# A triangle product's layer norm in a pipeline of its own, and the output units' first thirteen steps made within it

## The chip, the cores and the metric

The kernel runs on one core of a Trainium2 chip. A core has a matrix engine (TensorE, PE in the profile; its weight loads are PEld), VectorE (DVE), ScalarE (ACT), GpSimd (POOL) and SyncE (SP, which here only issues transfers), and 16 DMA engines. Each engine works through its own list of instructions in order; an instruction that waits holds up all behind it on its engine. SBUF is the on-chip memory of 128 partitions, PSUM the small accumulator memory in eight banks that TensorE writes. The metric is device microseconds (us) of one execution, as the median of several runs.

## The reference

Everything is float32; x is 1 x 512 x 512 x 64. Layer 0 is a gated triangle product, layer 1 a Fourier filter of 12 x 12 modes:

```python
xn = _ln(_gn(x), norm_w, norm_b)
left  = (xn @ left_w  + left_b)  * mask * sigmoid(xn @ lgate_w + lgate_b)
right = (xn @ right_w + right_b) * mask * sigmoid(xn @ rgate_w + rgate_b)
out_gate = sigmoid(xn @ ogate_w + ogate_b)
out = einsum('bkjd,bkid->bijd', left, right)        # per channel: a 512 x 512 product over k
out = _ln(out, onorm_w, onorm_b) @ out_w + out_b    # norm over the 64 channels
x = x + out * out_gate
x = x + spectral_filter(_gn(x))
```

The mask is the outer product of a 0/1 row of length 512 with itself, so only rows and columns that it keeps (at most K = 256 of them here) take part in the product; elsewhere the norm of zeros leaves only a bias row.

## The kernel before, in words

The kernel is one function, compact (L633). It has these stages, by the times of its profile: the statistics of the first group norm and the gather of the kept columns (to about 160 us); the gated left and right sides (to some 425 us); the triangle product channel by channel (425 to 591 us, L995, stored to DRAM as tri_d, L1003); then the loop of L1288, which the change rewrites (593 to some 1410 us); and the inverse transform with the final output (to the end).

The loop of L1288 runs over steps s, from -13 to 335. k = s // 8 and n = s % 8. It is one pipeline for two kinds of work:

- **Product steps**, s = 0 to 63. A step takes 1024 tokens, as 128 partitions by 8 groups of 64 channels. centered (L1143) multiplies a piece of the product with the matrix both, whose left half subtracts the channel mean and whose right half is the output projection (y_ps, L1153, sixteen matmuls). ScalarE squares the centered half into sq_c (L1173) and copies the projected half to SBUF (xt_c, L1174). VectorE sums the squares of two steps (summed, L1178) into PSUM. Once per eight steps ScalarE takes the root (L1184, in step n = 5) and VectorE its reciprocal (L1358, n = 7). VectorE multiplies the projected tokens with it (L1366), GpSimd adds the bias row for two steps at a time (L1373), and SP stores the pair, 512 KB, to u_d in DRAM (L1378).
- **Unit steps**, s = 64 to 319: 32 output units of eight steps. A unit is 64 columns by 128 rows of x, gathered earlier (L649). TensorE transposes (t_ps, L1133), ScalarE subtracts the group mean into xt_c (L1135), TensorE makes the centered values (c_ps) and the output gate (w_ps, both L1140); ScalarE squares (L1171), VectorE sums (L1178), and root and reciprocal follow as above. VectorE scales the gate (L1369) and adds its bias (L1375), ScalarE takes the sigmoid (L1316), GpSimd multiplies with u, read back from u_d, or with the bias row where the mask is 0 (gated, L1204), and adds x (added, L1208). VectorE takes the statistics for the second group norm (L1263), and TensorE begins the Fourier transform (L1235).

In every turn of the loop the early part of a step (transpose of step s + 13, centering, square and sum of step s + 12) is issued beside the late part (scaling) of step s. LEAD = 13 is that distance, for both kinds. So the first 13 turns only fill the pipeline with product steps, and during the last 12 product steps the early part already belongs to the units.

The whole block is in a manual schedule: each engine gets its instructions in the order in which the program issues them. The sums, the factors (reciprocals) of the product, the bias rows for VectorE and the group sums all lie in one PSUM tile, scratch, which is one bank (L1101). The projected values and the units' two results have two PSUM buffers each; the product's pool of PSUM is closed and replaced by the units' pools at s = 52 (L1302).

The queue of SP carries, in order, the loads of the product (load_product, L1121, 512 KB for two steps, four buffers) and the stores of u. The load for pair q is issued three pairs ahead of its projection. After the last store, load_u (L1195) reads u back for each second unit in 32 transfers of 64 KB.

The SBUF area xc is divided into eight places of 16 KB per partition: places 0, 1, 3 hold the first three units, which were gathered long before; place 6 holds the product's four load buffers; places 5 and 6 later hold u; places 4 and 2 the fourth and fifth unit; place 7 is free until the first unit's transform is saved.

Of the kernel before, what the change touches and what calls it, by code (L numbers as in the profile page):

```python
# [9 lines left out]
F32 = mybir.dt.float32  # L10
I32 = mybir.dt.int32
AF = mybir.ActivationFunctionType
ALU = mybir.AluOpType
# [33 lines left out]
def conv_preact_kernel(ctx: ExitStack, tc: tile.TileContext, t: dict):  # L47
# [585 lines left out]
    def compact(fc):  # L633
# [324 lines left out]
        with held:  # L958
# [59 lines left out]
            LEAD = 13  # L1018
            RING = 5
# [3 lines left out]
            with tc.manual_schedule(), tc.tile_pool(name="late", bufs=1) as lp:  # L1023
# [63 lines left out]
                with tc.tile_pool(name="np_x", bufs=LEAD + 2) as tp, tc.tile_pool(name="np_q", bufs=2) as sqp, tc.tile_pool(  # L1087
# [20 lines left out]
                    factors = [scratch[:, i, SIZE * 8 :] for i in range(2)]  # L1108
# [16 lines left out]
                    def transpose(s):  # L1125
                        k, n = divmod(s, SIZE)
                        if k < first:
                            return
# [14 lines left out]
                    def centered(s):  # L1143
                        if s >= first * SIZE:
                            return times(ps_c, "c_ps", s, center_x)
# [8 lines left out]

                        xts[s] = tp.tile([P, 4, P], F32, name="xt_c")
                        return ps

                    def raw(s):
                        return xts[s].rearrange("p h (i c) -> p (h i) c", c=C).rearrange("p (h i) c -> p h i c", h=2)
# [5 lines left out]
                    def squared(s, cps):  # L1165
                        n = s % SIZE
                        if n % 2 == 0:
                            sqs[s // 2] = sqp.tile([P, 16, C], F32, name="sq_c")
                        sq = sqs[s // 2][:, 8 * (n % 2) : 8 * (n % 2) + 8, :]
                        if s >= first * SIZE:  # L1170
                            nc.scalar.activation(sq, cps, AF.Square)  # L1171
                        else:
                            nc.scalar.activation(of_pair(sqs[s // 2], n % 2), cps[:, :, :, :C], AF.Square)  # L1173
                            nc.scalar.copy(raw(s), cps[:, :, :, C:])  # L1174
# [112 lines left out]
                    loaded = 0  # L1287
                    for s in range(-LEAD, total_g + 2 * SIZE):  # L1288
# [5 lines left out]

                        while loaded < K // 8 and 2 * loaded - LEAD - 5 <= s:
                            load_product(loaded)
                            loaded += 1
# [3 lines left out]
                        if s + LEAD - 1 == first * SIZE:  # L1301
                            products.close()  # L1302
                            ps_c = products.enter_context(tc.tile_pool(name="np_c", bufs=2, space=PSUM))
                            ps_w = products.enter_context(tc.tile_pool(name="np_w", bufs=2, space=PSUM))
                        if 0 <= s < total_g:
                            wps = raw(s) if k < first else times(ps_w, "w_ps", s, gate_x)
                            del xts[s]
                        if 0 <= s + LEAD - 1 < total_g:
                            cps = centered(s + LEAD - 1)
# [7 lines left out]
                        if n == 5 and 0 <= k + 1 < first + len(units):  # L1317
                            root(k + 1)
# [36 lines left out]
                        if 0 <= s + LEAD - 2 < total_g and (s + LEAD - 2) % 2 == 1:  # L1355
                            summed(s + LEAD - 2)
                        if n == 7 and k + 1 in rss:
                            nc.vector.reciprocal(factors[(k + 1) % 2] if k + 1 < first else rss[k + 1], rss[k + 1])  # L1358
                        if wps is not None:
# [3 lines left out]
                            if k < first:  # L1363
                                rs = factors[k % 2][:, 16 * c : 16 * c + 16].rearrange("p (h e i) -> p h e i", h=2, e=2)
                                rs = rs[:, :, odd].unsqueeze(3).to_broadcast([P, 2, 4, C])
                                nc.vector.tensor_mul(of_pair(z, odd), wps, rs)  # L1366
                            else:
# [261 lines left out]
```

## Time and profile before

| what | value |
|---|---|
| median of 3 runs | 1745.74 us (1744.92 to 1746.58) |
| the profiled execution itself | 1740.37 us |
| its span, first to last instruction | 1738.6 us |
| mean granted TensorE clock | 0.899 |
| busy over the span: PE, DVE, ACT, POOL | 1534.2, 1410.2, 949.4, 933.2 us |
| product projections y_ps, first and last start | 597.1 and 692.4 us |
| product scaling L1366, first and last start | 616.5 and 711.7 us |
| units' first centering c_ps, first gate w_ps | 693.8 and 710.9 us |
| units' scaling L1369, first and last start | 713.6 and 1406.8 us |
| product: sum L1178, scaling L1366, reciprocal of 64 columns L1358 | 1.21, 0.68, 0.56 us each |
| product: square L1173, copy L1174, root L1184 | 0.60, 0.59, 0.31 us each |
| bias addition on GpSimd L1373, 32 of them | 2.37 us each |
| load of two product steps, issue to landing | 6.4 us (median) |
| store of a pair of u, issue to landing | 2.6 us (median) |

A row of the profile's groups gives the line, engine, operation, the tile written and the tiles read, the count, the busy time and the mean of one, and the idle time of the engine just before, with what ended it. Two neighbouring instructions on one engine may overlap by a few tenths of a us at their ends, so the distance from start to start, read in order of time, is the better price of an instruction on a busy engine. The times of windows and timelines count from the span's start.

### The profile page before, as it was taken

To read this page: it belongs to the slowest core of one execution; us is meant where nothing else is said; L and a number is where in the kernel's file an instruction comes from. 1 tells how busy PE (TensorE), PEld (TensorE's weight loads), DVE (VectorE), ACT (ScalarE), POOL (GpSimd) and SP (SyncE) were. 2 spreads that over 40 slices of the span, in tenths; PEclk is the share of its full clock that TensorE was granted. 3 is DMA by queue.
4 is the path that set the end of the run, shared out by engine and by line. 5 is a ranking of instruction groups with operands and counts; after the bars stand their busy time and mean duration, and the time that the engine had idled before them with its cause. 6 is when DMAs were issued, how large, how long until landed. Compare 5 with 4: busy or idle time off the path is not lost. (4 is left out here: it accounts for less than half of the span.)

```text
span 1738.6 us, 32562 instructions
## 1 busy us (share of the span) xinstructions
PE 1534.2 (88%) x10926; PEld 1232.6 (71%) x10926; DVE 1410.2 (81%) x2967; ACT 949.4 (55%) x1740; POOL 933.2 (54%) x695
## 2 busy tenths in 40 slices
PE   6877899998999877999999999999999868998771
PEld 6776666655999766988888988898889735664340
DVE  7999788886555488899999999999999976785441
ACT  3766777764333377877777777777777632101000
POOL 4666111110000068799999999999999871111110
PEclk9999999999999899999999999999999876555555
DMA  7999378877999689577777767777777699999998
GB/s 293 420 419 418 85 240 285 300 243 288 306 304 301 234 280 331 180 264 264 247 249 262 250 242 249 262 249 246 248 267 245 200 341 423 426 426 426 426 428 363
DMA packets 189330, 518.48 MB, mean 298 GB/s; under 512 B 36416, under 2 KB 103232, under 8 KB 146272
## 3 DMA queue, kind: packets, MB, share of 16 engines
q1 hardware_dynamic: 154864, 295.71, 47.0%
q0 software_dynamic: 30816, 218.38, 33.9%
q10 hardware_dynamic: 3472, 2.20, 0.5%
q8 instruction: 89, 1.46, 0.3%
q14 instruction: 89, 0.73, 0.1%
HBM read 311.60 MB, written 204.60 MB: 297 GB/s over the span
## 5 line engine op out<-in xcount | busy, mean ns | idle before, releaser
L1140 PE MATMUL w_ps<-gate_x,xt_c 128*128 128x128 f32 x2048 | 280.3, 281 | 31.2 <-DVE z_t L1369 29.6
L1208 POOL TENSOR_TENSOR xc<-xc,z_t 128x1024 f32<-128x1024 f32 x127 | 301.2, 2372 | 8.0
L1140 PEld LDWEIGHTS w_ps<-gate_x,xt_c 128*128 128x128 f32 x2048 | 252.1, 194 | 47.7 <-DVE z_t L1369 46.0
L1140 PE MATMUL c_ps<-center_x,xt_c 128*128 128x128 f32 x2048 | 276.8, 279 | 1.2 <-ACT xt_c L1174 0.6
L1140 PEld LDWEIGHTS c_ps<-center_x,xt_c 128*128 128x128 f32 x2048 | 252.8, 194 | 3.6 <-ACT xt_c L1135 2.5
L1535 PE MATMUL l_ps<-xc,rinv 24*128 24x512 f32 x512 | 206.1, 1096 | 32.5 <-DVE xc L1542 20.4
L1263 DVE BATCH_NORM_STATS2 stats2c<-xc 128x6 f32<-128x128 f32 x1024 | 220.5, 278 | 8.5 <-POOL xc L1208 8.5
L1178 DVE TENSOR_REDUCE scratch<-sq_c 128x16 f32<-128x1024 f32 x160 | 194.5, 1216 | 23.4 <-ACT sq_c L1173 18.8
L1316 ACT ACTIVATE z_t<-z_t 128x1024 f32<-128x1024 f32 x128 | 135.5, 1059 | 133.4 <-DVE z_t L1375 132.7
L1373 POOL TENSOR_TENSOR z_t<-z_t,bias_row_out 128x1024 f32<-128x1024 f32 x32 | 75.7, 2367 | 241.9 <-DMA xc<-tri_d 220.7
L1535 PEld LDWEIGHTS l_ps<-xc,rinv 24*128 24x128 f32 x512 | 118.5, 296 | 114.9 <-DVE xc L1542 61.7
L1135 ACT ACTIVATE xt_c<-t_ps,ab_xc 128x512 f32<-128x512 f32 x256 | 175.9, 687 | 9.6 <-PE t_ps L1133 8.7
L1369 DVE TENSOR_TENSOR z_t<-w_ps,rs_n 128x512 f32<-128x512 f32 x256 | 172.0, 672 | 4.5 <-PE w_ps L1140 4.4
L1171 ACT ACTIVATE sq_c<-c_ps 128x512 f32<-128x512 f32 x256 | 150.5, 588 | 29.4 <-PE c_ps L1140 28.9
L1375 DVE TENSOR_TENSOR z_t<-z_t,scratch 128x1024 f32<-128x1024 f32 x128 | 156.3, 1221 | 10.7 <-ACT rs_n L1184 3.7
L1204 POOL TENSOR_TENSOR z_t<-z_t,xc 128x1024 f32<-128x1024 f32 x64 | 151.6, 2368 | 15.0 <-ACT z_t L1316 14.8
L777 DVE BATCH_NORM_STATS2 stats1c<-x_ps 128x6 f32<-128x512 f32 x256 | 156.2, 681 | 3.3 <-PE x_ps L776 2.9
L1133 PE MATMUL t_ps<-c_ident,xc 128*128 128x128 f32 x1024 | 157.4, 276 | 0.0
L1542 DVE TENSOR_TENSOR xc<-xc,l_ps 128x512 f32<-128x512 f32 x176 | 110.5, 682 | 55.6 <-DMA xc<-x_h,dst_i 47.0
L1133 PEld LDWEIGHTS t_ps<-c_ident,xc 128*128 128x128 f32 x1024 | 117.6, 141 | 51.6 <-issue 51.3
L1204 POOL TENSOR_TENSOR z_t<-z_t,bias_row_out 128x1024 f32<-128x1024 f32 x63 | 150.0, 2381 | 6.2 <-ACT z_t L1316 6.0
L751 ACT COPY xc<-xg 128x128 f32 x352 | 105.0, 298 | 51.6 <-DMA xg<-in_x,src_i 40.7
(231 smaller groups left out, 2540.8 us busy)
## 6 DMA issues: line engine op xcount, KB each, us to landing
x_h<-xc SPq DMA_DIRECT2D x64, 1024.0 KB, 8.1
out_x<-xc SPq DMA_DIRECT2D x44, 1024.0 KB, 32.5
sides_d<-o_c SPq DMA_DIRECT2D x64, 512.0 KB, 5.7
xc<-u_d SPq DMA_DIRECT2D x512, 64.0 KB, 2.4
out_x<-lx_t SPq DMA_DIRECT2D x20, 1024.0 KB, 39.5
left_raw<-sides_d SPq DMA_DIRECT2D x64, 256.0 KB, 4.4
right_raw<-sides_d SPq DMA_DIRECT2D x64, 256.0 KB, 4.2
tri_d<-tri_t SPq DMA_DIRECT2D x64, 256.0 KB, 3.6
```

Of the source, the lines that this page charges most:

```text
L777: nc.vector.bn_stats(stats[:, 0, 16 * (jc % quarter) + 4 * r + c, :], ps.rearrange("p i k -> p (i k)"))
L1133: nc.tensor.transpose(tps[:, i, :], flat[:, o : o + P], ident)
L1135: nc.scalar.activation(xts[s], tps, AF.Identity, bias=ab1[:, 2:3])
L1140: nc.tensor.matmul(ps[:, 2 * i : 2 * i + 2, :], xts[s][:, i, :], w, start=True, stop=True)
L1171: nc.scalar.activation(sq, cps, AF.Square)
L1178: nc.vector.tensor_reduce(totals[k % 2][:, 8 * (n - 1) : 8 * (n + 1)], sqs.pop(s // 2), AX.X, ALU.add)
L1204: nc.gpsimd.tensor_mul(zs[k, c], zs[k, c], u)
L1208: nc.gpsimd.tensor_add(xr, xr, zs.pop((k, c)))
L1263: nc.vector.bn_stats(st[k // 4][:, g, k % 4, :], x_of(k)[:, :, 2 * g : 2 * g + 2])
L1369: nc.vector.tensor_mul(z[:, 8 * odd : 8 * odd + 8, :], wps, rs)
L1375: nc.vector.tensor_add(z, z, bias_ps["ogate"].unsqueeze(1).to_broadcast([P, 16, C]))
L1535: nc.tensor.matmul(ps.rearrange("p j o -> p (j o)"), rinv[h, b, :], it[h], start=True, stop=True, tile_position=(32 * g, 0),)
```

## The change

The product steps leave the common loop and get one of their own, with steps p from -6 to 63:

- The projection of step p + 6 is issued beside the scaling of step p (LATE = 6 instead of 13). ScalarE copies the projected half into one of eight buffers in place 4 (tokens) and the scaled results are made in places 2 and 5 (scaled, four buffers of two pairs).
- The root and the reciprocal are made for four steps at a time (ROOT = 4), on 32 columns: the root is issued at the start of steps p = -1, 3, 7 and so on, the reciprocal at the end of the same steps. Sums and factors have two buffers each, all in the same PSUM tile, scratch.
- A store takes four steps (1 MB) instead of two and is issued three steps after their last scaling step; the last one follows the loop.
- Of the units' thirteen early steps, four (transpose, centering, square, sum) are made ahead of the loop, with centering in the buffers of the projection; eight within it, two in each of four groups of sixteen steps, with centering in the buffers of the transposes; and the thirteenth is only transposed, at p = 58. The squares of these steps go to place 7.
- The first unit's root is issued at p = 26 and its reciprocal at p = 29.

The old loop then begins at s = 64, with its pipeline already full, and does only unit steps; their code is otherwise the same.

```diff
+            LATE = 6
+            ROOT = 4
...
-                    factors = [scratch[:, i, SIZE * 8 :] for i in range(2)]
+                    sums_p, factors = [
+                        [scratch[:, i, (SIZE + ROOT * j) * 8 : (SIZE + ROOT * (j + 1)) * 8] for j in range(2)] for i in range(2)
+                    ]
+                    tokens = place(4).rearrange("p n c -> p (n c)")
+                    tokens = [tokens[:, i * N : (i + 1) * N].rearrange("p (h i c) -> p h i c", h=2, c=C) for i in range(8)]
+                    scaled = [place(i)[:, r * JC : (r + 1) * JC] for i in (2, 5) for r in range(2)]
+                    squares = [place(7)[:, 16 * i : 16 * i + 16] for i in range(4)]
...
+                    def squared_pair(p, ps):
+                        if p % 2 == 0:
+                            sqs[p // 2] = sqp.tile([P, 16, C], F32, name="sq_c")
+                        nc.scalar.activation(of_pair(sqs[p // 2], p % 2), ps[:, :, :, :C], AF.Square)
+                        nc.scalar.copy(tokens[p % 8], ps[:, :, :, C:])
+
+                    def begin_lead(o):
+                        transpose(first * SIZE + o)
+
+                    def end_lead(o, ps):
+
+                        ps = ps.rearrange("p i k -> p (i k)").rearrange("p (n c) -> p n c", c=C)
+                        s = first * SIZE + o
+                        for i in range(4):
+                            nc.tensor.matmul(ps[:, 2 * i : 2 * i + 2, :], xts[s][:, i, :], center_x, start=True, stop=True)
+                        squared(s, ps)
+                        if o % 2:
+                            summed(s)
+
+                    def product_step(p):
+
+                        steps = first * SIZE
+                        y = p + LATE
+                        ps = pair_of(y) if y < steps else None
+                        m, i = divmod(p - 2, 16)
+                        o = 2 * (m + 2)
+                        lead = 0 <= m < 4
+                        if lead and i in (0, 2):
+                            begin_lead(o + i // 2)
+                        if p == 58:
+                            begin_lead(LEAD - 1)
+                        g, at = divmod(p + 1, ROOT)
+                        if at == 0 and 0 <= g < steps // ROOT:
+                            rss["p"] = small.tile([P, ROOT * 8], F32, name="rs_p", bufs=2)
+                            nc.scalar.activation(rss["p"], sums_p[g % 2], AF.Sqrt, bias=eps, scale=1.0 / C)
+                        if ps is not None:
+                            squared_pair(y, ps)
+                        if lead and i in (2, 4):
+                            end_lead(o + i // 2 - 1, ps_t.tile([P, 4, P], F32, name="t_ps"))
+                        if p == 26:
+                            root(first)
+                        if p == 29:
+                            nc.vector.reciprocal(rss[first], rss[first])
+                        if (y - 1) % 2 and 0 <= y - 1 < steps:
+                            j = (y - 1) // 2
+                            nc.vector.tensor_reduce(
+                                sums_p[j // 2 % 2][:, 16 * (j % 2) : 16 * (j % 2) + 16], sqs.pop(j), AX.X, ALU.add
+                            )
+                        if p >= 0:
+                            j = p // 2
+                            z = scaled[j // 2 % 4][:, 16 * (j % 2) : 16 * (j % 2) + 16]
...
+                            nc.vector.tensor_mul(of_pair(z, p % 2), tokens[p % 8], rs.unsqueeze(3).to_broadcast([P, 2, 4, C]))
+                            if p % 2:
+                                nc.gpsimd.tensor_add(z, z, rows_of["out"].unsqueeze(1).to_broadcast([P, 16, C]))
+                        if at == 0 and 0 <= g < steps // ROOT:
+                            nc.vector.reciprocal(factors[g % 2], rss.pop("p"))
...
-                    loaded = 0
-                    for s in range(-LEAD, total_g + 2 * SIZE):
+                    for q in range(4):
+                        load_product(q)
+                    begin_lead(0)
+                    begin_lead(1)
+                    for o in range(4):
+                        end_lead(o, ps_y.tile([P, 2, 4, P], F32, name="y_ps")[:, 0])
+                        if o < 2:
+                            begin_lead(o + 2)
+                    loaded = 4
+                    for p in range(-LATE, first * SIZE):
+                        while loaded < K // 8 and 2 * (loaded - LATE) <= p:
+                            load_product(loaded)
+                            loaded += 1
+                        product_step(p)
+                        if p % 4 == 2 and p >= 6:
+                            store_product((p - 6) // 4)
+                    store_product(first * SIZE // 4 - 1)
+                    products.close()
+                    ps_c = products.enter_context(tc.tile_pool(name="np_c", bufs=2, space=PSUM))
+                    ps_w = products.enter_context(tc.tile_pool(name="np_w", bufs=2, space=PSUM))
+
+                    for s in range(first * SIZE, total_g + 2 * SIZE):
```

## The prediction

> **What bounds the kernel now.** I read the busy times by stretch first, around the stage that the change rewrites.
>
> ```profile
> 592.00:597.00 5.00, 0.00 (x0) 0.00 (x0) 0.00 (x0) 0.00 (x0) 0.00 (x0) 0.52 0.67 219
> 597.00:602.00 5.00, 4.86 (x45) 4.89 (x47) 0.40 (x1) 2.10 (x4) 0.00 (x0) 0.50 0.68 261
> ...
> 640.00:652.00 12.00, 7.82 (x126) 7.17 (x124) 10.77 (x14) 8.51 (x17) 9.45 (x5) 1.00 0.97 337
> ...
> 692.00:712.00 20.00, 18.83 (x169) 17.97 (x168) 17.27 (x22) 16.66 (x31) 15.40 (x7) 1.00 0.43 171
> ```
>
> The columns are PE, weight loads, DVE, ACT, POOL, clock, DMA share, GB/s. Nothing computes from 592 to 597 us; then VectorE is the busiest computing engine (10.8 of 12 us). The DMA share of 0.97 looks like a second limit, but it must be held against the order of time (start, length, engine, line, operation; in brackets the idle time before it and who ended it):
>
> ```profile
> 645.05 1.23 DVE L1178 TENSOR_REDUCE scratch<-sq_c 128x16 f32<-128x1024 f32 x1
> ...
> 646.37 0.69 DVE L1366 TENSOR_TENSOR z_t<-xt_c,scratch 128x512 f32<-128x512 f32 x1
> 647.09 0.31 ACT L1184 ACTIVATE rs_n<-scratch,eps 128x64 f32<-128x64 f32 x1 [0.38 <-DVE z_t L1366]
> ...
> 647.44 0.69 DVE L1366 TENSOR_TENSOR z_t<-xt_c,scratch 128x512 f32<-128x512 f32 x1 [0.38 <-ACT rs_n L1184]
> ...
> 648.23 1.23 DVE L1178 TENSOR_REDUCE scratch<-sq_c 128x16 f32<-128x1024 f32 x1
> ...
> 650.27 0.56 DVE L1358 RECIPROCAL scratch<-rs_n 128x64 f32<-128x64 f32 x1
> ...
> 651.65 1.23 DVE L1178 TENSOR_REDUCE scratch<-sq_c 128x16 f32<-128x1024 f32 x1
> ```
>
> VectorE hardly ever waits for data. From sum to sum a plain pair of steps takes 2.70 us (642.35 to 645.05), the pair with a root 3.18, the pair with a reciprocal 3.42. Eight steps are 2 x 2.70 + 3.18 + 3.42 = 12.0, and 64 are 96.0; measured, from 615.24 (the sum of step 0) to 712.44, it is 97.2. So VectorE sets this stage, and 1.2 us of stray waits are left over.
>
> The root is a lock: ScalarE's root waits for VectorE's product of the step before, and VectorE's next product waits for the root. The waits from 597 to 692 us say it is regular:
>
> ```profile
> DVE scratch L1178 <- ACT sq_c L1173: 18.8, 8, 10.8
> ...
> ACT rs_n L1184 <- DVE z_t L1366: 3.0, 6, 1.1
> ...
> DVE z_t L1366 <- ACT rs_n L1184: 2.3, 6, 0.4
> ```
>
> The 18.8 us lie almost all in the fill (10.8 us of it before the first sum at 601.60).
>
> What passes the stage on to the end is GpSimd:
>
> ```profile
> 712.47 2.37 POOL L1373 TENSOR_TENSOR z_t<-z_t,bias_row_out 128x1024 f32<-128x1024 f32 x1 [0.75 <-POOL z_t L1373]
> 718.88 2.37 POOL L1204 TENSOR_TENSOR z_t<-z_t,bias_row_out 128x1024 f32<-128x1024 f32 x1 [4.04 <-ACT z_t L1316]
> ...
> 740.43 0.88 DVE L1263 BATCH_NORM_STATS2 stats2c<-xc 128x6 f32<-128x128 f32 x4 [3.27 <-POOL xc L1208]
> ```
>
> From 718.88 GpSimd works without a gap to 764, and VectorE, after 740.43, is full to the end of the output units (98 of 100 us in 800 to 900). So the end moves by what the start of GpSimd's first gate, 718.88, moves. That start follows VectorE's first gate product (713.57) by 5.31 us: two products, the bias, table load 1.28, sigmoid 1.06.
>
> **The change, part by part,** as shifts of VectorE's chain, against the profiled execution.
>
> *The fill.* First products: 616.50 now. In the new order the first root follows four steps, and six are projected ahead. The lead steps 0 to 3 run in the hole: TensorE is free at 589.9; four steps of transposes (0.60) and centering (1.06), alternating with ScalarE's identity and square, end near 596.9 by my chaining, under the first load, which lands at 597.1. At nothing, then; if that cover were gone, step 0 would slip with it. The granted clock matters here: rows show 0.50 from 593 until 602.4, after TensorE's hole. With work in the hole I take 1.00, so projected step 0 ends at 598.3 rather than 599.3, step 1 at 599.3, and so on at the 1.0 to 1.3 us per step that two PSUM buffers allow. Square 4 starts at 602.95, its copy hands over at 603.95, table load to 605.25, root, square 5 at 605.46 to 606.06. Step 0's sum starts at 606.1 instead of 615.24: **-9.1 us**. (At half clock: -7.1.)
>
> *Sums.* From step 0's sum to the first gate product VectorE did 32 pairs of 2.70 and one more sum for the units, the one at 712.44. Now two product sums (1.31 each, with the gap to the product) lie ahead of step 0 and four for the units are in the loop: +2 x 1.31, less the 1.13 at 712.44. **+1.5**.
>
> *Roots.* 16 small roots lie behind step 0's sum with the one for the first unit, where there were 8: 15 x 0.45 + 0.6 (the unit's root, to which ScalarE comes late) against 8 x 0.48 = **+3.5**. It is 0.45, since 32 columns shorten the root's 0.31 by some 0.03 (a 128x32 copy takes 0.21). The lock has no data behind it: the root reads sums, the products read factors. "PSUM — Partial Sum Buffer" of the Trainium skill, section "PSUM bank collisions raise a hardware error", says that two engines must be kept apart in one bank even when both read; the 0.38 us waits agree. That rule speaks against this change: all sums and factors stay in one bank, so twice the roots is twice the locks. Were only data to count, this term would fall away.
>
> *Reciprocals.* 15 of 32 columns and one of 64, against 8 of 64. Not shown for 32: bounds are 0.06 (a 128x1 memset) and 0.56 (the 64). Half the columns over a fixed 0.06 would be 0.31, over the 0.16 of a 128x1 product 0.36; I take 0.34, with its gap 0.37. 15 x 0.37 + 0.67 against 8 x 0.72: **+0.5**. At 0.56 it would be +3.8.
>
> *The lead in the loop.* Here is the new wait. In steps 6, 22, 38 and 54, VectorE's first instruction is the unit's sum; it waits for ScalarE's square, which stands behind all that ScalarE does since the root of steps 3, 19, 35 and 51. Starts follow each other on ScalarE by 0.21 (root), 0.50 and 0.47 (square, copy), 0.57 (identity), 0.48 (unit's square). From root to the second unit square: 0.21 + 0.97 + 0.57 + 0.97 + 0.48 + 0.97 + 0.97 = 5.14, plus 0.60 to its end: 5.8 from the end of VectorE's product. VectorE has until then the locked product (ends 1.06), reciprocal (1.40), sum, two products: free at 4.2. It waits 1.6 us, four times: **+6.4**. Queued behind that sum are the next product sum and product, for which GpSimd waits; it has slack (2.37 of 5.4 us). All other squares come in time: after a root the next sum's square is done at 0.84, the sum can start at 1.45.
>
> *Edits at nothing.* TensorE: 1.06 per step and 3.3 per two lead steps, under 6 us per four steps. GpSimd: the same 32 additions. Sixteen stores of 1 MB instead of 32 of half: SP issues the loads as before three pairs ahead, but a store now waits for an addition two steps earlier, so loads stand less behind it; cover some 10 us for a landing of 6.4. Bytes are the same over a longer stretch. The 23.7 us that TensorE waited for loads are no gain to come, since VectorE, which sets the stage, waited for next to none of it; a loss would begin where a landing takes over 10 us. The last store lands later (1 MB: 3.6 plus some 1.3), then 32 reads of 0.36: ready near 738, wanted by unit 1's first gate near 743; without that 5 us cover each us counts.
>
> *Behind.* First gate products contiguous: 5.1 instead of 5.31, **-0.2**. TensorE is two steps ahead then, which GpSimd's gapless run hides.
>
> Sum: -9.1 + 1.5 + 3.5 + 0.5 + 6.4 - 0.2 = 2.6; of the 1.2 us of stray waits I take off 0.3, for loads that stand freer: **+2.3 us**. Span 1738.6 + 2.3 = 1740.9; the execution lies 1.77 above its span: 1742.7. The median of before is 5.4 above its profiled execution, so 1748.0.
>
> At the fill the rule of "TensorE: Matmul & The Clock Gate", section "Part 1: The HAM clock gate", is worth weighing: an idle window of about 3.4 us halves the clock. Rows: idle from 589.9, 0.59 at 592, full again 5.3 us after work began. By the rule the lead work keeps the clock; by the row of 626 to 630 (0.57 after TensorE was busy 1.8 of 4 us) it may not, and the sum would be 2.0 higher.
>
> **Rivals.**
> 1. *ScalarE is paced by TensorE after the root* (slower). In the fill, with two PSUM buffers, a step takes ScalarE 1.175 us (2.35 per two), not 0.97. If it does so in the four steps before the unit's second square, each wait grows by 4 x 0.205 = 0.8: +3.3, 1751.3. Decides once TensorE isn't two steps ahead at the root. Against it: while ScalarE waits, TensorE should fill both buffers. On this side too: a reciprocal at its upper bound (1751.3).
> 2. *ScalarE isn't held at the root,* so the unit squares come early: 6.4 less, 1741.6; if VectorE isn't held by the root either, 16 x 0.35 less again, 1736. Against it stand six waits in each direction.
> 3. *The fill isn't shortened*: the lead work begins only when the product's last stores have landed (594.5) and pushes step 0 by 3.5 us: 1751.5.
>
> **How the numbers follow.** A measurement of this kernel can tell about 0.2%, 3.5 us, from no change. Forecast +2.3, within that: 0.42 (own range 1744 to 1749). Rival 1: 0.26, rival 3: 0.08, both slower. Rival 2: 0.24, faster. The range 1739 to 1753 reaches below 1741.6 by half of what the root's hold on VectorE is worth, and above 1751.3 by the half clock's 2.0; it leaves out 1736 and the sum of several upper bounds.
>
> **What would show it.** Step 0's product near 607 and the first gate of GpSimd near 721; 16 waits of some 0.35 us of VectorE for the small root; four waits of about 1.6 us of VectorE's sum for the unit's square; clock 1.00 at 597. I am wrong if GpSimd's first gate starts before 717 or if the output units no longer follow it one to one.

## The result and the profile after

The changed kernel takes 1755.55 us (median of 8 runs, 1751.06 to 1760.39), the kernel before beside it 1745.44 us: a ratio of 1.0062, 95% interval 1.0041 to 1.0084. Measured a second time (after_again below) the ratio is 1.0049 (1.0030 to 1.0068). So the change costs some 9 to 11 us by the ratios (10.1 and 6.8 by the medians), where 2.3 were predicted. The time lies above the range; the median of the second measurement, 1750.09 us beside a kernel before of 1743.33, lies in it, so the change of the time is the better measure. The profiled execution takes 1753.33 us, its span is 1751.5 us. Its stages ahead of the change end 1.18 us later than in the profile of before (the last product tile is written out by 592.01 us instead of 590.83). Times of two profiles are therefore compared below from that point on; a shift with no other word is one of these.

The busy times by stretch of after, to be held against those of before (PE, weight loads, VectorE, ScalarE, GpSimd, granted clock, DMA share, GB/s):

```profile
592.00:597.00 5.00, 1.65 (x14) 1.65 (x15) 0.01 (x1) 1.72 (x3) 0.00 (x0) 1.00 0.44 122
597.00:602.00 5.00, 5.00 (x60) 4.75 (x58) 2.30 (x2) 3.69 (x8) 0.00 (x0) 1.00 0.89 350
...
620.00:624.00 4.00, 1.97 (x32) 1.78 (x32) 3.14 (x3) 0.72 (x3) 0.58 (x1) 1.00 0.92 340
624.00:628.00 4.00, 2.79 (x26) 2.79 (x28) 3.56 (x5) 2.77 (x7) 2.36 (x1) 0.55 0.38 154
...
640.00:652.00 12.00, 9.03 (x118) 8.02 (x116) 8.92 (x11) 7.81 (x17) 7.09 (x3) 0.99 0.95 347
692.00:712.00 20.00, 14.54 (x199) 12.98 (x198) 15.97 (x22) 14.06 (x30) 12.38 (x7) 1.00 0.70 260
```

The hole from 592 to 597 is filled in part, and the clock is full at 597. But VectorE, busy 10.8 of the 12 us from 640 before, is now busy 8.9 of them: it waits. The order of time shows for what:

```profile
617.56 0.62 ACT L1169 ACTIVATE xc<-t_ps 128x512 f32<-128x512 f32 x1
...
620.02 0.60 ACT L1169 ACTIVATE xc<-t_ps 128x512 f32<-128x512 f32 x1
...
620.66 1.23 DVE L1238 TENSOR_REDUCE scratch<-xc 128x16 f32<-128x1024 f32 x1 [2.51 <-ACT xc L1169]
...
623.18 0.69 DVE L1224 TENSOR_TENSOR xc<-xc,scratch 128x512 f32<-128x512 f32 x1
623.91 0.29 ACT L1205 ACTIVATE rs_p<-scratch,eps 128x32 f32<-128x32 f32 x1 [3.28 <-DVE xc L1224]
...
624.23 0.69 DVE L1224 TENSOR_TENSOR xc<-xc,scratch 128x512 f32<-128x512 f32 x1 [0.35 <-ACT rs_p L1205]
...
625.21 7.05 PE L1157 MATMUL y_ps<-both,xc 64*128 64x128 f32 x66 [3.24 <-ACT xc L1175]
```

VectorE's sum for the unit (L1238) waits 2.51 us for ScalarE's second unit square. ScalarE, once past it, waits 3.28 us at the next root for VectorE's product, TensorE 3.24 us for ScalarE, and the clock falls to 0.55. This happens four times; from 592 to 720 us the mean clock is 0.89, in before 0.95. The waits of the stage, from 608 us to the first gate product (us in all, times, longest):

```profile
DVE scratch L1238 <- ACT xc L1169: 7.9, 4, 2.5
...
DVE xc L1224 <- ACT rs_p L1205: 5.5, 15, 0.5
```

From the first sum of step 0 (609.29) to the first gate product (720.58) it is 111.3 us, where it was 98.3: +13.0. With the fill, 7.1 shorter, the first gate product comes 5.8 later and GpSimd's first gate 4.7 later. What follows is not in the prediction (VectorE's last four products and GpSimd first, then SP's own queue):

```profile
718.18 2.48 DVE L1224 TENSOR_TENSOR xc<-xc,scratch 128x512 f32<-128x512 f32 x4
717.84 7.01 POOL L1226 TENSOR_TENSOR xc<-xc,bias_row_out 128x1024 f32<-128x1024 f32 x3 [0.82 <-DVE xc L1224]
724.80 2.38 POOL L1264 TENSOR_TENSOR z_t<-z_t,bias_row_out 128x1024 f32<-128x1024 f32 x1
...
755.53 2.38 POOL L1264 TENSOR_TENSOR z_t<-z_t,xc 128x1024 f32<-128x1024 f32 x1 [3.36 <-DMA xc<-u_d]
...
779.27 0.98 POOL L649 DMA_INDIRECT xc<-in_x,src_i  x1 [5.85 <-DVE stats2c L1323]
```

```profile
720.23 4.98 SPq L1231 DMA_DIRECT2D u_d<-xc  x2
730.87 41.79 SPq L1255 DMA_DIRECT2D xc<-u_d  x64
772.76 3.41 SPq L1284 DMA_DIRECT2D x_h<-xc  x4
```

The same places in before:

```profile
718.56 42.68 SPq L1195 DMA_DIRECT2D xc<-u_d  x64
761.35 3.08 SPq L1224 DMA_DIRECT2D x_h<-xc  x4
```

```profile
766.16 0.98 POOL L649 DMA_INDIRECT xc<-in_x,src_i  x1 [2.06 <-PE w_ps L1140]
```

SP's list is, in order: the last store of the product, 32 reads of u for the first pair of units, 32 for the second, then the first unit's two stores. GpSimd's fifth load (L649 at 779.27; the first half of unit 5) goes into the place that those two stores read. The engine that the profile names as its releaser (VectorE's statistics; TensorE in other runs) had long been done: this is one of the waits for several semaphores where the last one is a transfer. The first unit's first store, issued at 772.76, has landed by 778.5; in before, issued at 761.35, by 765.4, just ahead of the load at 766.16. From the end of GpSimd's last bias addition on, the shift grows: addition +8.8, first read +11.1, fifth load +11.9, end +11.8. The first gate's +4.7 is no longer what the end follows. It has itself lost its old cause: at 724.80 it starts without idle time behind the last addition, and ScalarE's sigmoid, which it waited for in before, had ended at 724.21.

### The profile page after: what moved, and what is told of

It reads as the page before. It is cut to its first block, busy times and chain, and to the rows that moved or that the text cites. A ratio compares the mean times of both kernels' runs of the same rounds, so it can differ in the third digit from the quotient of the medians.

```text
span 1751.5 us, 32481 instructions
## 1 busy us (share of the span) xinstructions
PE 1564.9 (89%) x10926; PEld 1246.7 (71%) x10926; DVE 1408.6 (80%) x2975; ACT 952.0 (54%) x1748; POOL 933.4 (53%) x695
## 5 line engine op out<-in xcount | busy, mean ns | idle before, releaser
L1146 PE MATMUL c_ps<-center_x,xt_c 128*128 128x128 f32 x1952 | 264.8, 279 | 0.0
L1146 PEld LDWEIGHTS c_ps<-center_x,xt_c 128*128 128x128 f32 x1952 | 242.4, 195 | 2.1 <-ACT xt_c L1141 1.3
L1226 POOL TENSOR_TENSOR xc<-xc,bias_row_out 128x1024 f32<-128x1024 f32 x32 | 75.5, 2361 | 250.4 <-DVE xc L1224 242.7
L1169 ACT ACTIVATE sq_c<-c_ps 128x512 f32<-128x512 f32 x244 | 143.5, 588 | 31.6 <-PE c_ps L1146 31.2
L1264 POOL TENSOR_TENSOR z_t<-z_t,bias_row_out 128x1024 f32<-128x1024 f32 x63 | 149.6, 2375 | 2.1 <-ACT z_t L1389 1.4
L1238 DVE TENSOR_REDUCE scratch<-sq_c 128x16 f32<-128x1024 f32 x122 | 148.0, 1213 | 1.5
```

What stands on the lines that cost most here:

```text
L1146: nc.tensor.matmul(ps[:, 2 * i : 2 * i + 2, :], xts[s][:, i, :], w, start=True, stop=True)
L1169: nc.scalar.activation(sqs[s // 2][:, 8 * (n % 2) : 8 * (n % 2) + 8, :], cps, AF.Square)
L1238: nc.vector.tensor_reduce(totals[k % 2][:, 8 * (n - 1) : 8 * (n + 1)], sqs.pop(s // 2), AX.X, ALU.add)
L1264: nc.gpsimd.tensor_mul(zs[k, c], zs[k, c], u)
```

## The experiments

The table has all runs. Ratios are to the kernel before, run beside each; the last four columns are of the profiled execution, in us from the end of the last product tile's eviction. "Fifth load" is GpSimd's L649 of unit 5, "wait" what GpSimd waited there and, after the plus, at a gate for u; a wait under 0.2 is put as 0. The edits are shortened to what matters, and the comments in them are added.

| run | ratio (95%) | first gate | fifth load | wait | end |
|---|---|---|---|---|---|
| before | 1 | 128.1 | 175.3 | 2.1 | 1147.8 |
| after | 1.0062 (1.0041 to 1.0084) | 132.8 | 187.3 | 5.9 + 3.4 | 1159.5 |
| after_again | 1.0049 (1.0030 to 1.0068) | 135.2 | 188.2 | 7.9 | 1157.8 |
| late_sum | 0.9995 (0.9982 to 1.0007) | 125.2 | 180.0 | 6.2 + 3.3 | 1151.7 |
| sbuf_sums | 0.9988 (0.9977 to 1.0000) | 120.4 | 173.9 | 8.3 | 1146.5 |
| free_space | 1.0043 (1.0029 to 1.0057) | 135.2 | 189.4 | 6.0 + 2.9 | 1160.3 |
| small_store | 1.0046 (1.0030 to 1.0061) | 135.0 | 187.6 | 7.3 | 1158.7 |
| u_early | 1.0062 (1.0045 to 1.0078) | 132.8 | 186.0 | 8.0 | 1158.6 |
| pool_stores | 1.0044 (1.0028 to 1.0060) | 133.7 | 186.9 | 0 + 6.7 | 1158.4 |
| u_early_pool | 1.0049 (1.0032 to 1.0065) | 133.7 | 187.0 | 0 + 6.9 | 1162.3 |
| half_reads | 1.0013 (1.0003 to 1.0023) | 132.8 | 178.1 | 0 | 1148.9 |
| late_u | 1.0029 (1.0017 to 1.0040) | 133.6 | 179.0 | 0 | 1151.5 |
| before_pool | 0.9994 (0.9981 to 1.0007) | 129.8 | 176.4 | 0 | 1150.2 |
| more_reads (on before) | 1.0005 (0.9994 to 1.0015) | 127.9 | 177.5 | 1.1 + 3.3 | 1150.0 |
| before_late_u | 0.9988 (0.9979 to 0.9998) | 127.4 | 172.8 | 0 | 1146.3 |
| combined | 0.9906 (0.9892 to 0.9920) | 114.3 | 163.8 | 4.3 | 1137.0 |
| combined_late_u | 0.9891 (0.9874 to 0.9908) | 113.8 | 159.1 | 0 | 1135.5 |

In 15 of the 17 rows the end lies 970 to 974 us behind the fifth load, whatever was changed (the others, u_early_pool and combined_late_u: 975.3 and 976.4). Behind the first gate it lies 1016 to 1029 us. So of the points looked at the fifth load is the first that the end follows, and half_reads and late_u below test it; the rows differ in what brings GpSimd there late. The wait for u after the plus is no safe sign: after has it and after_again, the same kernel, has not, with all 7.9 us at the load.

**VectorE's terms**

*late_sum.*

```diff
- end_lead(o + i // 2 - 1, ps)              # sums at once, in step 16m + 6
+ end_lead(o + i // 2 - 1, ps, now=False)
...
+ if lead and i == 5:                       # end of step 16m + 7
+     summed(steps + o + 1)
```

> The unit's sum in the loop is put behind the product of the step after (16m+7 instead of 16m+6); nothing else moves. Theory: the wait of VectorE for ScalarE's square (7.9 us in four waits in the trace of after) is a place in VectorE's order and nothing more, and from the first sum to the first gate all is VectorE's chain; the waits go, the first gate of GpSimd comes 7 to 8 us earlier, and the end with it: about 1748, 7 to 8 us below after. Rival A: ScalarE (or TensorE at its half clock) cannot deliver that fast, and the wait comes back at the next root or the next product sum: less than 3 us below after. Rival B: the end is set by the read-back of the output units' u, not by the first gate; then the end still moves, since the last store moves as well, but by another amount than the gate.

The four waits are gone, and the first unit's root costs VectorE 0.38 us instead of 2.35. From the first sum to the first gate product it is 102.2 us (111.3). First gate 7.6 earlier, end 7.8 earlier, as the theory said. The ratio is 0.0054 to 0.0067 lower, 9 to 12 us. Rival A falls; rival B is answered further down.

*sbuf_sums.*

```diff
+ in_sbuf = lp.tile([P, 2, ROOT * 8], F32, name="in_sbuf")
+ sums_p = [in_sbuf[:, j] for j in range(2)]
```

> The product's sums lie in SBUF instead of the PSUM bank that also holds the factors; the arithmetic and the order are those of after. Theory: the root of four steps waits for the product ahead of it, and the product behind it waits for the root, only since all three touch one PSUM bank; 15 waits of 0.36 us of VectorE go (5.4 us), and ScalarE, let go about 1 us earlier, is less late at the four unit sums (2.0 us each, at most 1 us less): 6 to 9 us below after, 1746 to 1750. Rival: the root waits for data and place in the order, the bank is no matter: within 2 us of after.

End 13.1 earlier: more than expected, and by another sum. The waits of sbuf_sums, from 608 us to its first gate product:

```profile
DVE scratch L1240 <- ACT xc L1171: 13.2, 4, 3.3
ACT rs_p L1207 <- DVE in_sbuf L1218: 11.5, 7, 2.4
```

The product no longer waits for the root (5.45 us in after; 1.08 are left at the reciprocal): the lock was the bank that root and product shared, as the prediction said; both only read there, so no order of data asks for it. The rule of the Trainium skill that it weighed there ("PSUM — Partial Sum Buffer", "PSUM bank collisions raise a hardware error") agrees with these numbers. But the four unit sums wait 3.3 us each, not less than 2.0: VectorE, faster, comes earlier to a square that is no earlier. The rest is the pace of VectorE itself, taken from start to start without the waits: a product sum 1.31 us with its result in PSUM, 1.11 in SBUF (30 of them, -5.8), a product 0.685 and 0.641 (64, -2.8), a reciprocal 0.46 and 0.33 (15, -2.0). The stage has 98.9 us, 12.4 less than in after.

*free_space.* The tiles of the last four product steps before the stage are taken from place 5.

```diff
- out_t = op.tile([P, 2, K], F32, name="tri_t")
+ if c < C - 4: out_t = op.tile([P, 2, K], F32, name="tri_t")
+ else: out_t = places[:, o : o + 2 * K].rearrange("p (b i) -> p b i", b=2)
```

> The last four product tiles lie in a free part of the big tile, so that the lead work doesn't wait for their stores to land (7.9 us of ScalarE's wait at 594.6). The first sum of step 0 comes about 2 us earlier (the missing part of the 9.1 that the prediction counted on), and the end by the same: 1 to 3 us below after. Rival: the first projected step waits for its load (597) and for TensorE's clock anyway: within 0.7 us.

The rival. In after ScalarE's first lead instruction waits for the product's last stores, since its tile lies in SBUF where the stores' source was:

```profile
594.61 1.26 ACT L1141 ACTIVATE xt_c<-t_ps,ab_xc 128x512 f32<-128x512 f32 x2 [7.91 <-DMA tri_d<-tri_t]
...
600.19 2.06 PE L1157 MATMUL y_ps<-both,xc 64*128 64x128 f32 x32
```

In free_space that wait is gone and the lead work ends 3.0 us sooner, but the first projection then waits for its load:

```profile
599.84 4.45 PE L1161 MATMUL y_ps<-both,xc 64*128 64x128 f32 x48 [2.94 <-DMA xc<-tri_d]
```

It starts 8.2 us behind the last eviction, as in after, and step 0's sum 18.3 us behind it (after 17.3, after_again 18.7, before 24.4). The load is issued 4.5 us behind the last eviction, 2.5 in after and before: SP holds it until the product's last store has landed, 4.3 us after its issue at 591.66, where after needed 2.4. Why that store lands later is not known. The ratio cannot be told from after's.

**The way from the last store to the end**

*small_store.* store_product is called for each pair, 512 KB, three steps behind its addition.

> The product's result is stored as before the change, in 32 stores of 512 KB, each three steps behind its addition, instead of 16 of 1 MB. Theory: the second gate of GpSimd waits 3.4 us for the read-back of u because the last store of 1 MB lands 6.0 us after its issue (3.6 us for 512 KB in the trace of before); the wait falls to about 1 us, and the echo of it (3.7 us, VectorE's statistics and GpSimd's next load behind it) by as much: 3 to 5 us below after, 1750.5 to 1752.5, with the first gate where it was. Rival: the reads are late because of their own pace (0.65 us each), or the store's landing is not shorter: within 1.5 us of after.

The first read starts 4.8 us behind the last addition instead of 6.0, and there is no wait for u, but GpSimd's wait at the fifth load is 7.3 and the end is where it was: in time it cannot be told from after. The store's size is worth about a microsecond of landing. That the wait for u is missing is not shown to come from the store, since after_again has none either.

*u_early.*

```diff
- us[jc] = place(5 + jc % 2) ...
+ us[jc] = place(6 - jc % 2) ...
+ rows = other if jc == 0 else u_d     # other: sides_d, in the same shape
```

> The first 32 reads of u take rows of another tensor in DRAM that was written long before, into a part of SBUF that no late store reads; so they wait for no store of the product. (The first output unit's u is therefore other data than it should be; the work is the same.) Theory: the wait of GpSimd's second gate (3.4 us) goes, and with it all of the echo (3.7 us), since the echo is that same lateness passed to VectorE and back: 6 to 7.5 us below after, about 1748.5, with the first gate where it was. Rival A: the echo has a cause of its own (the order of the output units meets GpSimd's late start): 3 to 4 us below after. Rival B: something else is late at the same place and takes its turn: less than 2 us below after.

Rival B, and the theory fell: there is no wait for u, and the time does not move. GpSimd waits 8.0 us at the fifth load, as in after_again (7.9):

```profile
768.58 2.36 POOL L1266 TENSOR_TENSOR z_t<-z_t,bias_row_out 128x1024 f32<-128x1024 f32 x1
778.95 0.98 POOL L649 DMA_INDIRECT xc<-in_x,src_i  x1 [8.01 <-PE t_ps L1139]
```

SP's own rows of u_early:

```profile
714.90 11.25 SPq L1231 DMA_DIRECT2D u_d<-xc  x3
729.98 19.41 SPq L1257 DMA_DIRECT2D xc<-sides_d  x32
```

The reads began at 137.0 instead of 138.9: free of the store's data, they still stand behind the store in SP's list, and the store waits for GpSimd (issued at 725.82, 0.03 us behind the end of the last addition). From there to the first read it is 4.2 us, of which 3.4 go to two loads of the reads' places into SP's registers (L658, 2.16 and 1.27), which stand behind the store as well. In after the same two loads run while the store lands, so taking the landing away was worth only 1.8 us. This led to the theory of SP's queue.

*after_again, pool_stores, u_early_pool, before_pool.*

```diff
- nc.sync.dma_start(x1_h[...], x_of(k)[...])
+ (nc.gpsimd if k == 0 else nc.sync).dma_start(x1_h[...], x_of(k)[...])
```

> The changed kernel as it is, once more, beside the runs that are compared with it: 8 to 12 us above before.

> The changed kernel with one thing moved: the two stores of the first output unit's result are issued by GpSimd instead of SP, where they stand behind 64 reads of u. New theory: the third pair of loads of GpSimd (at 779.27 in after) goes into the place that these stores read, so it waits for SP's reads and not for GpSimd's own work; the lateness of the last store of the product (+8.8) reaches the end through SP's queue (reads 64 x 0.65, then the store, then the load). Once the stores stand on GpSimd's own queue that load comes when GpSimd gets to it, and the end is late by the first gate's 4.7 and by what the second gate's wait for u (3.4) adds: 3 to 4.5 us below after_again. Rival, the theory that u_early has shaken: the lateness comes over the second gate and VectorE alone: within 1 us of after_again, and GpSimd waits at that load as before.

> Both ways from the last store of the product to the end are cut: the first 32 reads of u take rows of another tensor, into a part of SBUF that no late store reads (the first output unit's u is other data than it should be), and the first unit's result is stored by GpSimd. New theory: only the first gate's lateness is left, +4.7 against before: 6.5 to 8 us below after_again. Rival: a third way exists (the units' order itself, TensorE's clock, the changed order of ScalarE): less than 4 us below.

> The kernel before with the same move of the first unit's two stores to GpSimd. If before already stood at the edge, with SP's queue and GpSimd's first gate both late by the same amount at the third pair of loads (GpSimd waits 2.06 us there), the time falls by 0 to 2 us; more than 3 us below before would mean that SP's queue bounded this stage before the change too, and that the prediction's reading of before (the end follows the first gate) was wrong from the start.

pool_stores shows the place right and the price wrong: the fifth load waits for nothing any more, but the gate for u now waits 6.70 us where it waited 3.36, and the end stays.

```profile
751.54 0.58 POOL L1284 DMA_DIRECT2D x_h<-xc  x1
752.14 2.37 POOL L1268 TENSOR_TENSOR xc<-xc,z_t 128x1024 f32<-128x1024 f32 x1
761.22 2.36 POOL L1264 TENSOR_TENSOR z_t<-z_t,xc 128x1024 f32<-128x1024 f32 x1 [6.70 <-DMA xc<-u_d]
...
779.25 0.98 POOL L649 DMA_INDIRECT xc<-in_x,src_i  x1 [0.15 <-PE t_ps L1139]
```

GpSimd's 1 MB store at 751.5 runs beside the reads that this gate waits for: the gate starts 9.3 us behind the issue of the 32nd read, 5.5 in after. In u_early_pool 32 reads take 22.0 us instead of 19.4, and the gate waits 6.85. So these two runs moved the collision and did not remove it; they do not tell queue from traffic. On before the same move costs or gains nothing that can be told.

*half_reads, more_reads.*

```diff
  for j, slot in enumerate(slots_of(mybir.EngineType.SP, jc)):
+     if jc < 2 and j % 2: continue          # half_reads, on after
...
+ if jc == 0: reads += reads[:8]             # more_reads, on before
```

> The changed kernel, with every second of the first 64 reads of u left out (the first two output units multiply by whatever lay in those rows; the work of all engines but SP is the same). Theory now: SP's queue is what carries the late last store of the product to the end; its 64 reads at 0.65 us, begun at 730.87 in after, make both the second gate's wait (3.4 us) and, since the first unit's stores stand behind them, the wait at the third pair of GpSimd's loads (5.9 us). With 32 reads fewer both waits go, and only the first gate's lateness is left: 5 to 7.5 us below after, 3 to 5 above before. Rival: SP's queue is beside the path, and what u_early and pool_stores left in place (order of VectorE, ScalarE and TensorE in the first output units) sets the end: within 1.5 us of after.

> The kernel before, with 8 of the first 32 reads of u made twice: 5.2 us more in SP's queue, nothing else. If before already stands at the edge of SP's queue (GpSimd waits 2.06 us at the third pair of loads, at 766.16), nearly all of it counts: 4 to 5.5 us above before. If before has the 5 us of cover that the prediction gave the reads: within 1 us of before.

half_reads is the first run that takes the lateness away: both waits are gone, with the first gate where it was in after. The fifth load is then 2.8 us later than in before, which is the first gate's 4.7 less the 2.1 that GpSimd waited there in before.

```profile
731.07 20.01 SPq L1257 DMA_DIRECT2D xc<-u_d  x32
751.18 17.04 SPq L1286 DMA_DIRECT2D x_h<-xc  x4
```

The stores follow the reads at 751 instead of 773, and the ratio falls from 1.0049 or 1.0062 to 1.0013. more_reads is inconclusive: the eight repeated reads took 2.5 us, not 5.2; the fifth load came 2.2 later and the profiled end 2.2 later, by the ratio the time is 0.9 longer (-1.0 to 2.6).

*late_u, before_late_u.*

```diff
- if n == 4 and v % 2 == 0 and 0 <= v < len(units) - 2:
+ if n == 4 and v % 2 == 1 and 0 <= v < len(units) - 2:
      load_u(v // 2 + 1)
```

> The changed kernel, complete, with one thing moved: from the second on, the 32 reads of u of a pair of output units are issued one unit later, behind the stores of the unit before instead of ahead of them. Theory: it is the place in SP's queue (first unit's stores behind 64 reads, GpSimd's third pair of loads behind these stores) and not the traffic of the reads that carries the lateness; the wait at that load goes, as in half_reads, though all 64 reads are made. The second gate's wait for u (3.4 us) stays, since the first 32 reads come no earlier, but is hidden or small: 4 to 7.5 us below after, ratio 0.9995 to 1.003. Rival: half_reads was faster because there was less traffic: within 2 us of after, ratio above 1.004.

> The kernel before with the same move. If before stood at the edge of SP's queue (GpSimd's wait of 2.06 us at the third pair of loads), 1 to 2.5 us below before; if the queue was covered there, within 1 us. Either way it says how much of the 11.9 us by which that load came later was free.

All reads and stores are there, in another order on SP, and both waits are gone:

```profile
733.69 18.39 SPq L1255 DMA_DIRECT2D xc<-u_d  x32
752.19 0.84 SPq L1284 DMA_DIRECT2D x_h<-xc  x2
761.17 20.92 SPq L1255 DMA_DIRECT2D xc<-u_d  x32
```

The fifth load comes at 179.0 instead of 187 to 189, the ratio falls to 1.0029: 3.5 to 5.8 us of the 9 to 11 are the place in SP's queue. The lower figure is not clear of noise by itself (late_u 1.0017 to 1.0040, after_again 1.0030 to 1.0068); the traces are clearer, with the end 6.3 to 8.0 earlier. Fewer reads are no rival for that part, since all are made. What the second gate's wait is worth cannot be read here, since after_again lacks it too. On before the move gains 2.1 us (0.3 to 3.7), and the 2.06 us of wait are gone: before had no cover at the fifth load, it was already some 2 us late there.

**Together**

*combined* has late_sum, sbuf_sums, small_store and free_space; *combined_late_u* has late_u's move as well.

> late_sum, sbuf_sums, small_store and free_space together. The waits at the unit sums (7.9), the locks at the roots (5.4), the late fill (2) and the larger landing (1.3) are all ahead of the last store of the product, so they should add up, whichever way the end is reached: 14 to 17 us below after, 5 to 7 us below before (about 1738, ratio 0.996 to 0.997). Rival: once VectorE is freed, ScalarE or TensorE sets the pace of the stage: no better than the best of the parts (within 2 us of sbuf_sums).

> combined with the same move. In combined GpSimd still waits 4.3 us at the third pair of loads, which follows SP's 64 reads and the stores by the same 45.8 us as everywhere; with the stores ahead of the second 32 reads this goes: 2.5 to 4.5 us below combined, ratio about 0.989. Rival: VectorE, full behind its first statistics, sets the end there: within 1 us of combined.

Both beat before: 1727.92 us and 1727.73 us, ratios 0.9906 and 0.9891. VectorE is busy 10.4 of 12 us again, about as in before (10.8), and TensorE 11.5 (combined):

```profile
640.00:652.00 12.00, 11.48 (x158) 10.60 (x160) 10.43 (x15) 10.27 (x22) 8.58 (x5) 1.00 0.98 344
```

From step 0's sum to the first gate product it is 91.9 us, 6.4 less than before the change; with the fill, the first gate comes 13.8 sooner than in before. The gain over after is larger than expected (14 to 17): 25 to 27 us by the ratios, 22.5 in the profile, where the four parts one by one give 21.0, 13.1 of it from sbuf_sums (6 to 9 expected). combined_late_u takes away the 4.3 us at the fifth load, which comes 4.7 earlier, but the end only 1.5 in the profile, and the two medians cannot be told apart. That is its rival: something other than this load now sets the end. What it is was not tested. (The 45.8 us of its expectation, from the first read to the fifth load, hold for combined; in after it is 48.4.)

## Why the prediction was wrong, by its own steps

**"So the end moves by what the start of GpSimd's first gate moves": this failed,** and with it the step "Edits at nothing". There the last store was priced (later, 4.9 us to land), 32 reads at 0.36 us were added, and 5 us of cover were found at unit 1's first gate. Four things were wrong. The last addition ends not with VectorE's last product but 4.2 us behind it (2.5 before), since the last four products come without sums between them and GpSimd's last three additions run back to back: the store is issued 8.8 later, where the gate is 4.7 later. The reads take 0.65 us each, in before already 0.67 (64 in 42.68 us); 0.36 is the length of the issuing instruction alone, without the register work between two of them. And there are 64 ahead of the first unit's stores. And the consumer that decides is not a gate but a load, two queues away: SP's reads, SP's store, GpSimd's load. There before had no cover (before_late_u): the prediction read that GpSimd works without a gap to 764, and the next instruction, at 766.16, is this load with its 2.06 us of wait. By half_reads and late_u this is worth 3.5 to 8.5 us of the 9 to 11. The prediction's own sign of being wrong, that the output units no longer follow the first gate one to one, came true.

**The first gate: +4.7, predicted +2.3.** Term by term, against the profile of after:

| step | predicted | measured |
|---|---|---|
| fill, step 0's sum | -9.1 | -7.1 (after_again -5.7) |
| stage in all: step 0's sum to first gate product | +11.6 | +13.0 (after_again +13.9) |
| lead in the loop: four waits | 6.4 (1.6 each) | 7.9 (2.5, then three of 1.8; 8.6 in after_again) |
| locks of 15 small roots | waits of some 0.35 each | waits of 0.36 each |
| lock of the first unit's root | 0.6 | 2.35 (2.25 in after_again, 0.72 in late_u) |
| reciprocal of 32 columns, from start to start | 0.37 us | 0.46 us (15: +1.4) |
| behind: first gate after first gate product | 5.1 us | 4.2 us (at once behind the last addition) |
| first gate of GpSimd | +2.3 | +4.7 |

- *Fill:* the clock was 1.00 at 597 as predicted; in after_again it was not (0.69 from 596 to 601). "At nothing, under the first load" was wrong in its cover: the lead work began at 594.6, when the product's last stores had landed. That is rival 3's mechanism, at 2.0 us of its 3.5. Yet taking the wait away (free_space) did not bring the 2 us: the load was then the last to come. What would be needed for -9.1 is open.
- *The lead in the loop:* right in place, number and kind (late_sum takes all four waits away). Three of the four waits are 0.2 over. The first is 0.9 over, and there ScalarE waits 0.68 us for TensorE's transpose (at 616.03), which is rival 1's mechanism. The low clock of 624 to 628 lies behind that wait and not ahead of it.
- *Roots:* the lock is the bank and is 0.36 us on average, as worked out (sbuf_sums). The first unit's root, priced at 0.6, follows the clock: ScalarE comes to it late where TensorE runs at half its clock behind the second wait for a unit's square. It cost VectorE 2.1 to 2.35 us in the six profiles of after's order in which that is so, and 0.72 in the three in which the clock is full there. The stretch ahead of the root in after and in late_u:

```profile
654.00:658.00 4.00, 4.00 (x41) 4.00 (x40) 1.71 (x3) 2.25 (x5) 3.26 (x2) 0.50 0.44 76
656.00:660.00 4.00, 3.41 (x52) 3.20 (x54) 3.05 (x6) 3.56 (x8) 3.04 (x2) 1.00 0.41 102
```

- *The clock rule:* the prediction weighed the idle window of about 3.4 us of "TensorE: Matmul & The Clock Gate" ("Part 1: The HAM clock gate") at the fill. The two profiles of the same kernel lie on its edge: after an idle 3.38 us the clock is 1.00 (after, 596 to 601), after 3.37 us it is 0.69 (after_again).

**Rivals.** 1 (slower, paced by TensorE) was right in direction, but it shows in one of the four waits only (two in after_again) and with less than half its size: 1.5 us of 3.3. 2 (not held at the root) was wrong. 3's mechanism is there in the fill, at 2.0 us. None of the three named SP's queue, where much of the loss lies; that the 1751.3 of rival 1 and the 1751.5 of rival 3 come near the second measurement's 1750.09 is luck.

## What to carry to other kernels

Before an end is said to follow one instruction, look for the first point behind which the time to the end is the same in nearly every run (here GpSimd's fifth load, 970 to 974 us ahead of the end in 15 of 17 profiles), and go back from it over every queue that feeds it, the ones that only issue transfers too: a store that waits for its data holds all that stands behind it on its queue. "DMA: Bandwidth & Descriptors" of the Trainium skill ("Anatomy of one DMA — SWDGE (gpsimd) path") says, where it describes GpSimd's path, that a wait is made on the issuing sequencer and not by the DMA engines; u_early shows it on SP's, with reads that needed nothing of the store and still were not issued before it, at 725.82. And a wait that vanishes from one instruction has to be looked for at the next one on the same engine before it is booked as a gain.

## What the runs showed of the hardware that was not expected

- VectorE's sum of 128x1024 into 128x16 takes 1.31 us from its start to the next instruction's when result and next operand share a PSUM bank, 1.11 us when the result lies in SBUF (after, sbuf_sums); the 15 reciprocals and 64 products of the stage gain as well (0.13 and 0.04 us each). The four unit sums, whose result stays in PSUM in both, go from 1.26 to 1.14 when the instruction behind them no longer touches that bank.
- SP issues 64 KB reads at register-held addresses at 0.57 to 0.75 us each on average over 32 (64 in 41.8 us in after), most of them 0.52 to 0.57 apart: 0.33 for the issue and the rest for the register work between. Bandwidth need not be short for that: from 765 to 775 us of u_early, where the reads run to 772.7, the DMA share is 0.33, at 95 GB/s.
- Two profiled executions of one kernel differ by 2.4 us at the first gate (132.8 and 135.2), 1.5 of it in the fill, where one has the full clock and the other 0.69. A shift of 1 or 2 us between two profiles shows nothing by itself.
